# A cross-attention and state-space kernel: the second transpose of 26 row-tile pairs is taken from TensorE and given to VectorE and DMA

## The chip, the cores and the metric

The kernel runs on one core of one Trainium2 chip. The metric is the device time of one execution in microseconds (us), lower is better. TensorE (PE) multiplies matrices and can also transpose; VectorE (DVE), ScalarE (ACT) and GpSimd (POOL) work on vectors; SyncE (SP) issues nearly all DMA transfers. Each engine works through its own queue in order, and a waiting instruction holds up all that stands behind it in that queue.

## The reference, cut to what matters

All arrays are fp32. T = 4096 query rows, S2 = 3202 key rows, H = 512, 8 heads of 64.

```python
x  = layernorm(builder_state, g1, beta1)          # 4096 x 512
base_n = layernorm(base_state, g1, beta1)         # 3202 x 512
x  = residual + mha(x, base_n, W_qkv, b_qkv, W_o, b_o)   # softmax attention, 8 heads
residual = x
xn = layernorm(x, g2, beta2)
U  = (xn @ W_in.T + b_in) @ Bmat                  # 4096 x 64
s_t = silu(s_{t-1} @ A.T) + U[t]                  # a scan over the 4096 rows
ssm_out = states @ Cmat
out = residual + ssm_out + (program_probs.mean(1) @ W_prog.T + b_prog)
```

Two steps need rows turned into columns, because a matmul contracts over partitions: the normalized query rows before the Q projection, and the normalized attention output (`xn`) before the product with W_in and Bmat.

## The kernel before, in words

A first stage (to about 216 us) normalizes the 26 chunks of keys, computes K and V for all heads and writes them to DRAM. Then comes the main stage: 8 blocks of 512 query rows (Q = 0..7), each with 4 head pairs (hp) and 2 halves of 256 rows, so 64 units. A unit goes through 13 steps of 256 keys. A step has eight 64x256 matmuls `s<-q,k` (`scores`, L639), one exponential on ACT (`weights`, L709), one addition into a running sum (`add`, L717, on DVE, or on POOL for steps 2, 6 and 10), and eight matmuls `po<-p,v` (`product`, L749). At the end of a unit POOL folds the sum (`fold`, L724), PE sums it over partitions (`sums`, tile pd, L767), and DVE inverts it (L802) and scales the output. The last 80 us or so hold the scan.

Beside the units run two chains per block, each in two pairs of 128-row tiles:

- `queries` (L866), for the block to come: load x, mean and variance on DVE (`stats`), factors on POOL, `scaled` on ACT (L855, tile xh), then `turn`: eight 128x128 PE transposes into two PSUM tiles (L282, tile tp_x) and two ACT copies to the tile xn (L305). Later, four `heads` pieces (L307) multiply xn by the Q weights: per head pair two accumulation groups of four 128x256 matmuls (L312).
- `project` (L914), for the block that has ended: load x, add a bias row on POOL, `outs` on PE (`pa`, L933), `x1` on DVE, `stats`, `factors`, `mod` on POOL (L947, the row that is stored), `scaled` on ACT, `store`, then `turn` (tile tp_y), two copies (L978) and `inputs`: eight 128x128 matmuls (tile pu, L984), whose result ACT writes to u (L992).

The order of each queue is not written by hand: class `Plan` takes pieces with an engine, an assumed cost in ns, the pieces they come after, a due time in steps of 2150 ns, and counted rings of buffers (`m` = 2 PSUM banks, `x` = 4 row tiles, `xn` = 2, `x1` = 2, ...). It plays the pieces through once and emits them in the order in which they start there. On the chip only that order and the semaphores remain. K and V loads are issued inside the `scores` pieces, 10 and 6 steps ahead; each waits until the buffer it takes (13 per kind) was last read. PE switches between 128-row work (`turn`, `heads`, `outs`, `inputs`) and 64-row work (`scores`, `product`, `sums`, `sample`); the planner charges each switch.

Of the kernel before, what the change touches and what calls it, by code (L numbers as in the profile page):

```python
# [20 lines left out]
P = 128  # L21
NC = H // P
NCH = 26
CK = 128
NDC = NCH // 2
# [144 lines left out]
def xattn_ssm_kernel(  # L170
# [117 lines left out]
    xnp = actx.enter_context(tc.tile_pool(name="xnp", bufs=2))  # L288
# [18 lines left out]
    def heads(Q, hp, xns):  # L307

        pq = m_tile([P, 512], f"pq_{Q}_{hp}")
        for half in range(2):  # L310
            for i in range(NC):
                nc.tensor.matmul(  # L312
                    pq[:, half * QU : (half + 1) * QU],
                    wq[:, i, hp * P : (hp + 1) * P],
                    xns[half][:, i, :],
                    start=(i == 0),
                    stop=(i == NC - 1),
                )
        yield
        t = qp.tile([P, QB], F32, tag="q", name=f"q_{Q}_{hp}")  # L320
        nc.scalar.activation(  # L321
            t, pq, AF.Identity, bias=bias[:, hp : hp + 1], scale=HD**-0.5
        )
        qt[Q, hp] = t

    first_xns = []

    def first_queries(x0):

        xns = []  # L330
        for half in range(2):
            xn = xnp.tile([P, NC, QU], F32, tag="xn", name=f"xn_0_{half}")
            xns.append(xn)
            for t in range(NT // 2):
                name = f"x{half * QU + t * P}"
                last = normalize(x0[:, half * (NT // 2) + t, :], P, name, later=True)
                yield
                yield
                xh = last()
                yield  # L340
                yield
                for _ in turned(xn, xh, t, name):
                    yield
                yield
                yield
        first_xns.extend(xns)
        pieces = heads(0, 0, xns)
        next(pieces)
        for _ in pieces:
            yield  # L350
        yield
# [422 lines left out]

    def output(w):
        Q, hp, half = w["at"]
        o = o_t[Q, hp, half] = op.tile([P, QU], F32, tag="o", name=f"o_{w['name']}", bufs=12)
        nc.scalar.copy(o, w["po"][:, 0, :QU])  # L778

    def join(w):  # L780
        o = o_t[w["at"]]
        nc.vector.tensor_tensor(o, w["po"][:, 1, :QU], o, ALU.add)  # L782

    def finish(w, i, d, plan):
# [5 lines left out]
        def denominators(k):  # L790
            if k == 0:
                w["rd"] = op.tile([P, QU], F32, tag="rd", name=f"rd_{name}", bufs=2)
            to = w["pd"][k][:, :QU] if k else w["rd"]
            nc.scalar.activation(
                to, w["pd"][k][:, :QU], AF.Copy, accum_out=rises[:, 3 * i + k : 3 * i + k + 1]
            )

        def whole():
            nc.vector.tensor_tensor(w["rd"], w["pd"][1][:, :QU], w["rd"], ALU.add)
# [35 lines left out]
    def norm_pieces(plan, ks, gets, d, after, names, gives):  # L835
# [21 lines left out]
        for t, (k, v) in enumerate(zip(ks, vs)):  # L857
# [5 lines left out]
                     [] if t else ["xh", "xh"], [("fs", (*k, "stats")), gives[t]])  # L863
        return vs

    def queries(plan, Q, d):  # L866

        xns, copied = [], []
        for half in range(2):
            ks = [("query", Q, half * 2 + t) for t in range(2)]  # L870
            at = [Q * QB + half * QU + t * P for t in range(2)]
            k2, vs, w = ("queries", Q, half), [{}, {}], {}

            def load(v, r):
                v["x"] = xp_.tile([P, H], F32, tag="x", name=f"x_{r}", bufs=4)
                nc.sync.dma_start(v["x"], x[r : r + P, :])

            for t in range(2):
                plan.add((*ks[t], "load"), "SP", 60, partial(load, vs[t], at[t]), [from_(d - 2 * STEP)],
                         d - 2 * STEP, ["x"])  # L880
            nv = norm_pieces(plan, ks, [lambda v=v: v["x"] for v in vs], d, [(*k, "load") for k in ks],
                             [f"x{r}" for r in at], [("x", (*k, "load")) for k in ks])

            def turn(half=half, nv=nv, at=at, w=w):
                xn = xnp.tile([P, NC, QU], F32, tag="xn", name=f"xn_{Q}_{half}")
                xns.append(xn)
                w["turns"] = [turned(xn, nv[t]["xh"], t, f"x{at[t]}") for t in range(2)]
                for one in w["turns"]:
                    next(one)

            plan.add((*k2, "turn"), "PE", 1050, turn, [(*k, "scaled") for k in ks], d + 4 * STEP,
                     ["m", "m", "xn"], [("xh", (*ks[0], "scaled"))])
            for t in range(2):
                plan.add((*ks[t], "copy"), "ACT", 560, lambda t=t, w=w: next(w["turns"][t], None),
                         [(*k2, "turn")], d + 5 * STEP + t, [], [("m", (*k2, "turn"))])
                copied.append((*ks[t], "copy"))
            d += 2 * QSTEP
        head_pieces(plan, Q, range(NC), xns, copied, d, QSTEP // 2,
                    [("xn", ("queries", Q, half, "turn")) for half in range(2)])

    def head_pieces(plan, Q, hps, xns, copied, d, apart, xn_):
        for hp in hps:
            v = {}

            def head(v=v, hp=hp):
                v["heads"] = heads(Q, hp, xns)
                next(v["heads"])

            plan.add(("heads", Q, hp), "PE", 3700, head, copied, d, ["m", "q"], xn_)
# [4 lines left out]
    def project(plan, Q, halves, d, index):  # L914

        for half in halves:
# [3 lines left out]
            now = plan.ALONE if Q == NQB - 1 else 0  # L920

            def load(v, r):
                v["x"] = xp_.tile([P, H], F32, tag="x", name=f"xr_{r}", bufs=4)
                nc.sync.dma_start(v["x"], x[r : r + P, :])
# [16 lines left out]
            def x1_(v, r):  # L941
                v["x1"] = xp_.tile([P, H], F32, tag="x1", name=f"x1_{r}")
# [10 lines left out]
            for t in range(2):  # L953
                plan.add((*ks[t], "load"), "SP", 60, partial(load, vs[t], at[t]), [from_(d - 4 * STEP)],
                         d - 4 * STEP + t, ["x"])
# [3 lines left out]
                     ["m", "m", "x1", "x1"], [("o_", ("output", i)) for i in units_])  # L959
            for t in range(2):  # L960
                plan.add((*ks[t], "x1"), "DVE", 680, partial(x1_, vs[t], at[t]), [(*k2, "outs")],
                         d + STEP + t, [], [("m", (*k2, "outs"))])
            nv = norm_pieces(plan, ks, [lambda v=v: v["x1"] for v in vs], d + STEP, [(*k, "x1") for k in ks],
                             [f"y{r}" for r in at], [("x1", (*k2, "outs"))] * 2)
            for t in range(2):
                plan.add((*ks[t], "mod"), "POOL", 1280, partial(mod, vs[t]), [(*ks[t], "x1")], d + 2 * STEP,
                         [], [("x1", (*k2, "outs"))])
                plan.add((*ks[t], "store"), "SP", 60, partial(store, vs[t], at[t]), [(*ks[t], "mod")],
                         d + 3 * STEP, [], [("x", (*ks[t], "load"))])
# [10 lines left out]
            def inputs(w=w, at=at):  # L980
                w["pu"] = m_tile([P, P], f"pu_{at[0]}")
                for c in range(NC):
                    for t in range(2):
                        nc.tensor.matmul(  # L984
                            w["pu"][t * NS : (t + 1) * NS], wc[:, c, :], w["xn"][:, t, c, :],
# [3 lines left out]
            def kept(t, w=w, at=at):  # L989
# [10 lines left out]
            plan.add((*k2, "turn"), "PE", 1050, turn, [(*k, "scaled") for k in ks], d + 5 * STEP - now,  # L1000
                     ["m", "m", "xn2"], [("xh", (*ks[0], "scaled"))])
            for t in range(2):
                plan.add((*ks[t], "copy"), "ACT", 560, partial(copy, t),
                         [(*k2, "turn")] + ([(*ks[0], "copy")] if t else []), d + 6 * STEP + t, [],
                         [("m", (*k2, "turn"))])
            plan.add((*k2, "inputs"), "PE", 700, inputs, [(*k, "copy") for k in ks], d + 7 * STEP - now,
                     ["m"], [("xn2", (*k2, "turn"))])
            for t in range(2):
                plan.add((*ks[t], "kept"), "ACT", 280, partial(kept, t), [(*k2, "inputs")],
                         d + 8 * STEP + t, [], [("m", (*k2, "inputs"))])  # L1010
# [53 lines left out]
    def last_fetch():  # L1064

        for g in range(2):
            r = LAST + g * P
            t = xp_.tile([P, H], F32, tag="x", name=f"xr_{r}", bufs=4)
            nc.sync.dma_start(t, x[r : r + P, :])
            xl.append(t)  # L1070

    def open_scan():
# [5 lines left out]
        one = xnp.tile([P, 8, NCK], F32, tag="xn", name="scan_1")  # L1078
# [4 lines left out]
        two = xnp.tile([P, 1024], F32, tag="xn", name="scan_2")  # L1083
# [175 lines left out]
    def last_rows(plan, d):  # L1259
# [9 lines left out]
        def x1_(g):  # L1269
            if g == 0:  # L1270
                wide()
            v["x1"][g] = xp_.tile([P, H], F32, tag="x1", name=f"x1_l{g}")
# [75 lines left out]
        for g in range(2):  # L1348
# [3 lines left out]
                     ["x1"] + ([] if g else ["p", "p"]))  # L1352
# [107 lines left out]
    def drain(plan):  # L1460
# [4 lines left out]
        plan.add("fetch", "SP", 500, last_fetch, stored + [("weights", n, NDC - 1)], d, ["x", "x"])  # L1465
# [9 lines left out]
        plan.add("c2", "SP", 200, open_scan, [("heads", NQB - 1, NC - 1)], a0 - 6 * STEP, ["xn", "xn", "q"])  # L1475
# [208 lines left out]
    with tc.manual_schedule():  # L1684
        for g in range(AHEAD_K):
            load_k(*steps[g])
        for g in range(AHEAD):
# [3 lines left out]
                s=2, m=2, mt=1, o=1, p=NP, acc=3, extra=4, q=6, x=4, x1=2, xn2=1, fs=2,  # L1691
                xn=2, xh=2, max=2, rd=2, o_=12,
            ),
            dict(q=[("heads", 0, 0)], xn=[("first", half) for half in range(2)]),
        )
        head_pieces(plan, 0, range(1, NC), first_xns, [], 4 * STEP, 4 * STEP,
                    [("xn", ("first", half)) for half in range(2)])
# [109 lines left out]
```

## Time and profile before

| | |
|---|---|
| median of 3 runs | 2023.07 us (2022.85 to 2023.64) |
| the profiled execution's own time | 2022.73 us |
| its span, first to last instruction | 2020.9 us |
| granted TensorE clock, mean | 0.995 |
| busy: PE, DVE, ACT, POOL | 1983.2, 1170.6, 1160.3, 789.3 us |
| PE transposes of x rows and of y rows (L282) | 128 and 120 instructions, 17.7 and 16.4 us busy |
| ACT copies of these (L305, L978) | 32 and 30, 17.3 and 16.1 us |
| DMA packets | 187030, 190.66 MB |
| K and V loads | 432 of 128 KB of each, median 2.2 us to landing |

A row of the profile's table of groups gives line, engine, operation, tiles (out<-in), shape, count, then busy us, mean ns of one instruction, then the engine's idle time before such instructions and what ended it. The engine-over-time view gives start, duration, engine, line, operation and count; the duration of a group of matmuls reaches to the modelled end of the last one, so the pace is read from the starts. fp32 matmuls stand as two instructions each in the trace, transposes as one.

### The profile page before, as it was taken

How to read it: one execution, taken by the hardware profiler on the slowest of the kernel's cores; microseconds unless marked ns; L12 is line 12 of the kernel's file. 1: busy time of each engine (PE TensorE's matmuls, PEld its weight loads, DVE VectorE, ACT ScalarE, POOL GpSimd, SP SyncE). 2: the span in 40 equal slices, each digit the busy share in tenths (PEclk: the TensorE clock that was granted, in tenths of full speed). 3: DMA queues.
4: the chain of work that ended last, by engine and by line, in shares of the span. 5: the costliest groups of instructions: out<-in, count | busy, mean ns of one | idle time of the engine just before them, and what ended most of it. 6: DMA issues, size and time to landing. Idle time of an engine off the chain costs nothing.

```text
span 2020.9 us, 66912 instructions
## 1 busy us (share of the span) xinstructions
PE 1983.2 (98%) x29534; PEld 1324.9 (66%) x29534; DVE 1170.6 (58%) x1481; ACT 1160.3 (57%) x1530; POOL 789.3 (39%) x631
## 2 busy tenths in 40 slices
PE   8999999999999999999999999999999999999996
PEld 4445676776677667766677667766776667766764
DVE  4321366566665666566656666566656665666575
ACT  2233566566665566556656666556655665665653
POOL 2111244235533453245523553345324552345424
PEclk9999999999999999999999999999999999999998
DMA  5632322122222322122222222232212322444475
GB/s 169 192 99 68 99 79 83 54 80 90 88 67 78 97 79 67 55 62 93 81 59 80 90 88 67 78 96 79 67 55 62 93 81 59 144 136 129 130 208 192
DMA packets 187030, 190.66 MB, mean 94 GB/s; under 512 B 20904, under 2 KB 160168, under 8 KB 186732
## 3 DMA queue, kind: packets, MB, share of 16 engines
q1 hardware_dynamic: 182184, 178.62, 29.4%
q10 hardware_dynamic: 4548, 7.67, 1.2%
q8 instruction: 235, 3.85, 0.8%
q14 instruction: 63, 0.52, 0.1%
HBM read 156.32 MB, written 29.88 MB: 92 GB/s over the span
## 4 chain that ended last, share of the span: by engine, by line
PE 78%; DVE 10%; POOL 7%; issue 3%; ACT 1%; DMA 1%; DVEq 0%; POOLq 0%; ACTq 0%
PE po L749 27%; PE s L639 27%; DVE acc L717 6%; PE pq L312 5%; PE pk L588 4%; PE pv L555 4%; POOL acc L717 4%; PE pa L933 4%; PE pd L767 1%; DVE rd L802 1%; ACT p L709 1%; PE tp_x L282 1%; DVE acc L703 1%; POOL acc L724 1%; PE sm L657 1%
## 5 line engine op out<-in xcount | busy, mean ns | idle before, releaser
L709 ACT ACTIVATE p<-s,shifts 128x1024 f32<-128x1024 f32 (+1 forms) x832 | 894.1, 1081 | 522.8 <-PE s L639 510.4
L717 DVE TENSOR_TENSOR acc<-p,acc 128x1024 f32<-128x1024 f32 (+1 forms) x515 | 620.0, 1204 | 406.9 <-POOL acc L717 310.6
L639 PE MATMUL s<-q,k 64*64 64x256 f32 x12800 | 841.4, 378 | 2.7 <-ACT p L709 1.1
L749 PE MATMUL po<-p,v 64*64 64x256 f32 x12800 | 823.2, 376 | 0.0
L717 POOL TENSOR_TENSOR acc<-p,acc 128x1024 f32<-128x1024 f32 x189 | 446.9, 2365 | 809.1 <-DVE acc L717 484.1
L639 PEld LDWEIGHTS s<-q,k 64*64 64x64 f32 x12800 | 483.9, 133 | 217.2 <-issue 21.4
L749 PEld LDWEIGHTS po<-p,v 64*64 64x64 f32 x12800 | 489.5, 133 | 189.0 <-issue 2.2
L724 POOL TENSOR_TENSOR acc<-acc 128x512 f32<-128x512 f32 x64 | 104.5, 1633 | 135.8 <-DVE acc L717 118.0
L717 DVE TENSOR_TENSOR acc<-p,p 128x1024 f32<-128x1024 f32 x64 | 84.6, 1322 | 60.1 <-ACT p L709 54.1
L312 PE MATMUL pq<-xn,wq 128*128 128x256 f32 x512 | 119.0, 385 | 0.0
L802 DVE RECIPROCAL rd<-rd 128x256 f32<-128x256 f32 (+1 forms) x65 | 112.4, 1729 | 2.2
L312 PEld LDWEIGHTS pq<-xn,wq 128*128 128x128 f32 x512 | 94.6, 190 | 23.2 <-issue 11.6
L933 PE MATMUL pa<-wo,o 128*128 128x512 f32 x240 | 107.0, 599 | 0.0
L782 DVE TENSOR_TENSOR o<-po,o 128x256 f32<-128x256 f32 x64 | 27.2, 424 | 128.4 <-ACT o L778 128.2
L555 PE MATMUL pv<-wv,ct 128*128 128x512 f32 (+1 forms) x208 | 96.4, 616 | 1.0 <-ACT ct L523 0.7
L588 PE MATMUL pk<-ct,wk 128*128 128x512 f32 (+1 forms) x224 | 88.8, 549 | 0.0
L321 ACT ACTIVATE q<-pq,bias 128x512 f32<-128x512 f32 x32 | 22.0, 687 | 108.6 <-PE pq L312 108.6
L933 PEld LDWEIGHTS pa<-wo,o 128*128 128x128 f32 x240 | 44.4, 190 | 56.0 <-issue 55.8
L703 DVE TENSOR_TENSOR acc<-x,acc 2x256 f32<-2x256 f32 x128 | 78.1, 610 | 3.0
L523 DVE COPY ct<-tp_c 128x512 f32<-128x512 f32 (+1 forms) x13 | 8.5, 651 | 105.9 <-PE tp_c L282 105.9
L555 PEld LDWEIGHTS pv<-wv,ct 128*128 128x128 f32 (+1 forms) x208 | 38.3, 193 | 44.5 <-issue 41.7
L588 PEld LDWEIGHTS pk<-ct,wk 128*128 128x128 f32 x224 | 39.2, 190 | 42.6 <-issue 42.6
(213 smaller groups left out, 1224.1 us busy)
## 6 DMA issues: line engine op xcount, KB each, us to landing
k<-kd SPq DMA_DIRECT2D x432, 128.0 KB, 2.2
v<-vd SPq DMA_DIRECT2D x432, 128.0 KB, 2.2
xr<-in_x_dram SPq DMA_DIRECT2D x32, 256.0 KB, 4.5
x1d<-xr SPq DMA_DIRECT2D x32, 256.0 KB, 2.2
x<-in_x_dram SPq DMA_DIRECT2D x28, 256.0 KB, 3.2
cx<-in_ctx_dram SPq DMA_DIRECT2D x25, 256.0 KB, 3.0
vd<-vs SPq DMA_DIRECT2D x25, 256.0 KB, 2.4
kd<-ks SPq DMA_DIRECT2D x48, 128.0 KB, 1.8
```

What stands on the lines that cost most here:

```text
L312: nc.tensor.matmul(pq[:, half * QU : (half + 1) * QU], wq[:, i, hp * P : (hp + 1) * P], xns[half][:, i, :], start=(i == 0), stop=(i == NC ...
L555: nc.tensor.matmul(pv[h * HD : h * HD + n, :H], ct[:, k, o : o + n], wv[:, k, :], start=(i == 0), stop=(i == NC // parts - 1), skip_group_ ...
L588: nc.tensor.matmul(pk[:, :n_g], wk[:, i, hp * P : (hp + 1) * P], ct[:, i, :n_g], start=(i == 0), stop=(i == NC - 1),)
L639: nc.tensor.matmul(s[k0 : k0 + HD, a, b, :], kts[(*w["at"][:2], c)][r, b * CK + k0 : b * CK + k0 + HD], q[r], start=True, stop=True, skip_ ...
L703: nc.vector.tensor_tensor(to[r], t[r], to[r], ALU.add)
L709: nc.scalar.activation(t[:, :, :nb, :], w["ps"][c][:, :, :nb, :], AF.Exp, bias=w["shift"])
L717: engine.tensor_tensor(w["acc"][:, :, :nb, :], t[:, :, :nb, :], before[:, :, :nb, :], ALU.add)
L724: nc.gpsimd.tensor_tensor(acc[:, :, 0, :], acc[:, :, 0, :], acc[:, :, 1, :], ALU.add)
L749: nc.tensor.matmul(w["po"][a * HD : (a + 1) * HD, k, :QU], vts[Q, hp, c][r, b, a * HD : (a + 1) * HD], t[r, a, b, :], start=(c == 0 and b ...
L782: nc.vector.tensor_tensor(o, w["po"][:, 1, :QU], o, ALU.add)
L802: nc.vector.reciprocal(w["rd"][:, part], w["rd"][:, part])
L933: nc.tensor.matmul(v["pa"], o_t[Q, c, half][:, t * P : (t + 1) * P], wo[:, c, :], start=(c == 0), stop=(c == NC - 1),)
```

## The change

For 26 of the 29 pairs that these chains handle in the main stage (the query pairs of blocks 1 to 6, and the output pairs of blocks 0 to 6), `turn` and the two copies are replaced. After `scaled`, two DVE instructions (`flip`) transpose each 128x512 tile in 32x32 blocks, from xh into the pair's own row tile (x or x1), interleaving the blocks of the two tiles. Then 16 DMA transfers on SP (four `move` pieces of four) carry blocks to their partitions: each takes 32 partitions x 4 x 64 numbers, that is 128 pieces of 256 bytes, 32 KB. The columns of xn (512 wide now, one tile for both halves) then stand in mixed order: 32 rows of the first tile, 32 of the second, and so on. `inputs` reads its columns with a stride to undo that; for the queries of blocks 1 to 6 the mixed order stays through scores, exponentials and products, and is undone where ACT and DVE read `po` and `pd` from PSUM (`output`, `join`, `denominators`, `whole`). `heads` has one group of four 128x512 matmuls in place of two groups of four 128x256. Row tiles are now kept in pairs (rings x = 2, x1 = 1, xn = 1: the same bytes), a row pair's `flip` also waits for both `mod` pieces, its `store` is planned after its `flip`, and `inputs` is due 16 steps after `outs` instead of 7. The query blocks 0 and 7 and the last block's output pair keep PE transposes.

```diff
-        for half in range(2):
-            for i in range(NC):
-                nc.tensor.matmul(
-                    pq[:, half * QU : (half + 1) * QU],
-                    wq[:, i, hp * P : (hp + 1) * P],
-                    xns[half][:, i, :],
+        for i in range(NC):
+            nc.tensor.matmul(
+                pq,
+                wq[:, i, hp * P : (hp + 1) * P],
+                xn[:, i, :],
...
+    def rows_of(w, t, of_queries=False):
+        if not mixes(w["at"][0]):
+            return t
+        return mixed(t, slice(None)) if of_queries else t.rearrange("p (t a r) -> p t a r", t=2, r=TB)
...
-        nc.scalar.copy(o, w["po"][:, 0, :QU])
+        nc.scalar.copy(rows_of(w, o), rows_of(w, w["po"][:, 0, :QU], True))
...
-            plan.add((*k2, "turn"), "PE", 1050, turn, [(*k, "scaled") for k in ks], d + 4 * STEP,
-                     ["m", "m", "xn"], [("xh", (*ks[0], "scaled"))])
-            for t in range(2):
-                plan.add((*ks[t], "copy"), "ACT", 560, lambda t=t, w=w: next(w["turns"][t], None),
+            if mixes(Q):
+                for t in range(2):
+                    plan.add((*ks[t], "flip"), "DVE", 720,
+                             lambda t=t, v=v, nv=nv: flip(v["x"], nv[t]["xh"], t),
+                             [(*k, "scaled") for k in ks], d + 4 * STEP + t, [], [("xh", (*ks[0], "scaled"))])
+                for a in range(P // TB):
+                    plan.add((*ks[0], f"move{a}"), "SP", 2600, partial(move_, a),
+                             [(*k, "flip") for k in ks] + ([(*ks[0], "move0")] if a else after),
+                             d + (5 + 4 * a) * STEP, [] if a else takes, [free])
...
+    def flip(pair, xh, t):
+        nc.vector.transpose(
+            pair.rearrange("p t h -> p (t h)").rearrange("p (g t r) -> p t g r", t=2, r=TB)[:, t],
+            xh.rearrange("p (g r) -> p g r", r=TB),
+        )
+
+    def move(xn, pair, a):
+        n = 2 * TB
+        of = pair[a * TB : (a + 1) * TB].rearrange("p t h -> p (t h)").rearrange(
+            "p (c b k) -> p b c k", b=P // TB, k=n
+        )
+        for b in range(P // TB):
+            nc.sync.dma_start(xn[b * TB : (b + 1) * TB, :, a * n : (a + 1) * n], of[:, b])
+
+    def mixed(of, t):
+        return of.rearrange("p (a t r) -> p t a r", t=2, r=TB)[:, t]
+
+    def mixes(Q):
+        return 0 < Q < NQB - 1
...
-                         [], [("x1", (*k2, "outs"))])
-                plan.add((*ks[t], "store"), "SP", 60, partial(store, vs[t], at[t]), [(*ks[t], "mod")],
+                plan.add((*ks[t], "store"), "SP", 800, partial(store, vs[t], at[t]),
+                         [(*ks[t], "mod" if last else "flip")], d + 3 * STEP, [], [("x", (*ks[0], "load"))])
...
-                            w["pu"][t * NS : (t + 1) * NS], wc[:, c, :], w["xn"][:, t, c, :],
+                            w["pu"][t * NS : (t + 1) * NS], wc[:, c, :],
+                            w["xn"][:, t, c, :] if last else mixed(w["xn"][:, c, :], t),
...
+                for t in range(2):
+                    plan.add((*ks[t], "flip"), "DVE", 720, lambda t=t, w=w, nv=nv: flip(w["x1"], nv[t]["xh"], t),
+                             [(*k, of) for k in ks for of in ("scaled", "mod")], d + 5 * STEP + t, [],
+                             [("xh", (*ks[0], "scaled"))])
+                for a in range(P // TB):
+                    plan.add((*ks[0], f"move{a}"), "SP", 2600, partial(move_, a),
+                             [(*k, "flip") for k in ks] + ([xn2] if a else []), d + (6 + 2 * a) * STEP,
+                             [] if a else ["xn2"], [("x1", (*k2, "outs"))])
```

## The prediction

> **What bounds the kernel now.** I read the page's totals first, then the PE idle time by engine waits, then PE's queue over time, and only then the other engines around the row pairs.
>
> From the page: the span, busy time by engine, and the 40 slices of PE and of its granted clock.
>
> ```profile
> span 2020.9 us, 66912 instructions
> ...
> PE 1983.2 (98%) x29534; PEld 1324.9 (66%) x29534; DVE 1170.6 (58%) x1481; ACT 1160.3 (57%) x1530; POOL 789.3 (39%) x631
> ...
> PE   8999999999999999999999999999999999999996
> ...
> PEclk9999999999999999999999999999999999999998
> ```
>
> PE is busy in nearly every slice at full clock; 30 of its 38 us of idle lie in the first 245 us and the last 61 (view by stage). In the main stage only one wait of PE's matmuls on another engine recurs, pd (the sum over partitions) waiting for POOL's fold, seen in the waits by PE and by its weight loads:
>
> ```profile
> PE pd L767 <- POOL acc L724: 4.9, 6, 0.8
> PEld pd L767 <- POOL acc L724: 11.0, 12, 1.3
> ```
>
> So PE work taken from the main stage should come off the end, unless it turns into a wait of that kind. The groups by shape that the change touches:
>
> ```profile
> L312 PE MATMUL pq<-xn,wq 128*128 128x256 f32 x512 | 119.0, 385 | 0.0
> L933 PE MATMUL pa<-wo,o 128*128 128x512 f32 x240 | 107.0, 599 | 0.0
> L282 PE MATMUL tp_x<-ident,xh_x 128*128 128x128 f32 x128 | 17.7, 279 | 0.0
> L282 PE MATMUL tp_y<-ident,xh_y 128*128 128x128 f32 x120 | 16.4, 280 | 0.0
> L305 ACT COPY xn<-tp_x 128x512 f32<-128x512 f32 x32 | 17.3, 588 | 1.7 <-PE tp_x L282 1.7
> ```
>
> **What goes: the PE transposes.** One `turn` in PE's queue over time:
>
> ```profile
> 914.88 1.91 PE L639 MATMUL s<-q,k 64*64 64x256 f32 x32
> 916.72 1.09 PE L282 MATMUL tp_y<-ident,xh_y 128*128 128x128 f32 x8
> 917.74 1.58 PE L639 MATMUL s<-q,k 64*64 64x256 f32 x24
> 919.13 1.04 PE L749 MATMUL po<-p,v 64*64 64x256 f32 x16
> ```
>
> Sixteen 64x256 records take 0.865 us where nothing interrupts, 0.054 each. So the first s ends at 914.88 + 32 x 0.054 = 916.61, and the second would have begun, counted back from po, at 919.13 - 24 x 0.054 = 917.83. The turn with both switches of tile size costs 1.22 us; another (931.4 to 932.6) costs 1.18. In the built order of PE the main stage holds 29 turns before and 3 after, and none shared its switches with other 128-row work, so 26 x 1.2 = 31.2 us go. That the transposes disappear is thus certain; only what follows is open.
>
> **`heads`.** A piece is 16 records in 3.65 us (pq from 810.53 to the next s at 814.18). Eight records of 128x512 at 107.0/240 = 0.446 us are 3.57; in one run of 16 pa records (902.47 to 909.53) they are 0.441, hence 3.53. I take 0.1 x 32 = 3.2 us.
>
> **`inputs`.** The same 16 records of 128 columns, read in runs of 32. Scan matmuls of 32 columns with a stride of 16 bytes (L1098 zl, 231 ns) last as long as the 64 contiguous ones of sm L676 (230 ns), so I take nothing; between 0 and double (14 x 1.0 us) lie the ends.
>
> **PE's added waits.** 20 matmuls (6 of `heads`, 14 of `inputs`) now wait for 6 to 8 DMA semaphores. Semaphore instructions on PE's queue last 51 ns at the median in the trace, so at most 20 x 7 x 0.051 = 7 us; the one product before with six waits (227.67) starts 0.05 us after the s work ahead of it (225.89 + 1.73), since PE's queue runs ahead of its array. I take 1.5.
>
> **Flips.** 52 DVE instructions on 128x512. Nearest rows with 512 elements per partition on DVE: bn_stats 673 to 695 ns, x1 681; the far end is three times that, as ACT's strided write of u (L992, 479 ns for 128 elements) is against its 364 for 256. I take 0.7: 36 us of DVE, which has 800 us idle. What matters is who stands behind a flip. In DVE's new order the row flips come after the ninth add, and the second query pair's flips right after its stats, ahead of adds 11 and 12, the fold and pd. In the trace DVE stands idle just there:
>
> ```profile
> 919.65 1.22 DVE L717 TENSOR_TENSOR acc<-p,acc 128x1024 f32<-128x1024 f32 x1 [5.43 <-POOL acc L717]
> ...
> 976.45 2.02 DVE L717 TENSOR_TENSOR acc<-p,acc 128x1024 f32<-128x1024 f32 x2 [4.21 <-ACT xh_x L855]
> ```
>
> First place: the second xh_y is ready at 916.15 (ACT 915.34 + 0.81), the flips run 916.2 to 917.6, and the add waits for POOL until 919.6 anyway. Only one stats of x now precedes the fold, so POOL reaches the fold some 2 us sooner, while PE reaches pd 1.5 us sooner (turn and inputs gone from between, 2.4; one scores group more, 0.86). Second place: four flips, POOL's factors and tenth add begin 1.45 us later (975.5), the flips of x end at 978.6 instead of add 11 starting at 976.45, and the fold ends near 981.8 against 979.8; pd stood at 983.49 and comes to about 982.0. Both are level within 0.5 us. I take 2 us for new pd waits in all, with ends of -5 (today's waits vanish) and +34 (26 pairs x today's longest, 1.3).
>
> The Trainium skill's page Vector Engine (DVE) Microarchitecture Reference, section 3.8, says the transpose mode sustains one element per cycle per lane. By the skill's 0.96 GHz that would be an estimated 0.53 us plus a start, the near end of these rows; no trace here shows it.
>
> **ACT.** 52 copies at 0.59 go (31 us); ACT waits 510 us for scores in the table of waits, so nothing is gained. `output` and `denominators` read PSUM in runs of 32: free, or at three times as much 48 x 0.75 us for each of three on ACT, which has 860 us idle. The two DVE reads, 0.42 each now, likewise fall in its idle.
>
> **Moves on SP.** 416 DMAs of 32 KB. SP's queue:
>
> ```profile
> 913.59 0.66 SPq L1021 DMA_DIRECT2D k<-kd  x1
> 914.34 0.41 SPq L1029 DMA_DIRECT2D v<-vd  x1
> 914.85 0.38 SPq L1021 DMA_DIRECT2D k<-kd  x1
> ```
>
> An issue costs 0.4 us, so 16 take 6.4; loads of 128 KB overlap although each lands 2.2 us after issue. Behind a waiting move stand K and V loads, whose buffers are free about 13 steps (28 us) before use: a block of SP of 11.8 us (the longest wait of `store` for POOL, L950) leaves PE untouched today. That wait shrinks, since `store` now stands after the flip. Between the last move's due time and its reader lie 4 steps (8.6 us) for `inputs` and 7 for `heads`. I take nothing.
>
> **Sum.** 2023.07 (the profiled execution, 2022.73, is 0.34 under the median) - 31.2 - 3.2 + 1.5 + 2 = **1992.2**, given as 1992.
>
> **Rivals.**
>
> *The flip is slow and DVE becomes the bound* (slower). Beside the second place's four flips there is no room left, at the others about 2 us. At 1.4 us a flip, 6 such places lose 2.8 us and the other 14 pairs up to 1.4: 36 us, which eats the gain (2028). At 2.1: 73 us, 2065. It decides from about 1.4 us on. For it: DVE is in order and pd already waits on that chain. Against it: all rows of 512 elements stay under 0.7.
>
> *The moves come late.* If the 16 went one after the other, each landing (2.2 us) before the next, a row pair would need 35 us where `inputs` is due 10 steps (21.5 us) after the first: 13.7 us x 14 = 192 us, about 2180. It decides from 1.34 us per move. Against: the loads above overlap. The skill's page DMA: Bandwidth & Descriptors (Rules for kernel authors) speaks for it: coalesce, transfers under 64 KB are mostly overhead. By that rule, 32 KB in 256-byte pieces is a poor transfer; the trace's smallest K loads (64 KB, 1.9 us) show only that such overhead is latency that overlaps.
>
> *Half the gain is given back in pd waits.* The full 7 us on semaphores and 1.3 us at each of 14 row pairs (18): 2023.07 - 34.4 + 25 = 2014.
>
> **Chances.** Forecast 0.72 (1982 to 2002: up 10 for the waits, down 10 for today's pd waits and idle at changed places); half given back 0.13 (2002 to 2019, of which 0.01 within 0.2%); slow flip 0.10, of which 0.03 within 0.2%; late moves 0.05. Within 0.2% (4 us, about what a measurement of this kernel can tell from no change) 0.04 in all, faster 0.84, slower 0.12. The range leaves out slow flips, late moves and little more: 1982 to 2015.
>
> **What would show it.** tp_x at 32 and tp_y at 8 records; PE busy down by about 34 us; pq at 256 records near 0.445 us; flips near 0.7 us; pd waits on POOL near today's 11 us; moves issued at 0.4 us and K loads without a wait on PE's side. Wrong if flips exceed 1.4 us, if pu or pq waits for DMA, or if pd's waits grow by tens of us.

## The result, and the profile after

The changed kernel takes 2033.59 us (median of 5 runs, 2031.61 to 2036.71), against 2023.07 before: a ratio of 1.0052 with a 95% interval of 1.0038 to 1.0067. It is slower by half a per cent, where 1992 was forecast. The profiled execution took 2036.71 us, 3.1 above the median; before's lies 0.3 below its own, so the profiles differ by 14.0 us and the medians by 10.5.

The page of the changed kernel (span, busy time, PE over 40 slices, TensorE's granted clock, DMA packets):

```profile
span 2034.9 us, 66527 instructions
...
PE 1967.0 (97%) x29070; PEld 1258.4 (62%) x29070; DVE 1210.8 (60%) x1533; ACT 1134.3 (56%) x1478; POOL 796.7 (39%) x631
...
PE   8999999999999999999999999999999999989996
...
PEclk9999999999999999999999999999999999999998
...
DMA packets 246935, 204.28 MB, mean 100 GB/s; under 512 B 80809, under 2 KB 220073, under 8 KB 246637
```

PE's busy time fell by 16.2 us, half of what was expected, and one slice (1781 to 1831 us) now shows an 8. The clock row is the same as before: what is lost below is too short to show in slices of 51 us. The groups that the change touches, by shape (busy us, mean ns of one | idle time of the engine before them):

```profile
L312 PE MATMUL pq<-xn,wq 128*128 128x512 f32 x256 | 118.3, 605 | 0.0
L932 DVE STREAM_TRANSPOSE x<-xh_y 128x512 f32<-128x512 f32 x28 | 18.2, 690 | 15.8 <-ACT xh_y L857 15.8
L932 DVE STREAM_TRANSPOSE x<-xh_x 128x512 f32<-128x512 f32 x24 | 15.6, 689 | 22.8 <-ACT xh_x L857 19.3 <-DMA v<-vd 3.4
L283 PE MATMUL tp_x<-ident,xh_x 128*128 128x128 f32 x32 | 4.8, 278 | 1.5 <-ACT u L1051 1.5
L283 PE MATMUL tp_y<-ident,xh_y 128*128 128x128 f32 x8 | 1.3, 286 | 0.0
```

The transposes are gone as planned, and a flip takes 0.69 us. But DVE stood still before flips for 38.6 us. PE's waits in the main stage of the changed kernel (us in total, times, longest):

```profile
PE s L635 <- ACT p L705: 15.6, 17, 2.7
PE pd L763 <- POOL acc L720: 9.8, 4, 6.9
PE pu L1042 <- DVE x L1000: 4.8, 1, 4.8
PE pu L1042 <- DMA xn<-x: 4.5, 2, 3.2
```

Before, only pd had 4.9 us and s 1.1. To put this into one account I summed the gaps between PE's matmul records from 216 to 1945 us, and took the time at which the last scores matmul ends (1955.1 us before, 1969.2 after). PE's gaps grew from 8.5 to 38.8 us (+30.3). And the trace's clock records show something that the kernel before never had in this stage: six stretches, 27.3 us in all, at half the TensorE clock. PE was busy for 23.5 us of them, so 11.7 us are lost. With 30.3 + 11.7 lost and an end 14.1 us later, PE's own work fell by 27.9 us. Two such stretches, as busy time of PE, PEld, DVE, ACT and POOL in a window, with the granted clock ahead of the last two columns. The records give 941.9 to 945.3 us for the first and 1829.4 to 1836.2 for the second; the windows reach a little beyond, hence 0.53:

```profile
942.10:945.50 3.40, 3.40 (x40) 2.12 (x36) 2.06 (x3) 1.11 (x1) 1.26 (x2) 0.53 0.32 58
...
1829.00:1836.00 7.00, 3.77 (x36) 2.29 (x40) 5.81 (x8) 1.73 (x5) 4.54 (x2) 0.53 0.03 9
```

**A gap that comes once per block.** SP's queue of the changed kernel, between the two loads of one query pair (start, duration, count):

```profile
899.43 0.38 SPq L880 DMA_DIRECT2D x<-in_x_dram  x1
...
913.92 3.29 SPq L944 DMA_DIRECT2D xn<-x  x4
...
919.31 2.52 SPq L944 DMA_DIRECT2D xn<-x  x4
...
924.15 6.13 SPq L944 DMA_DIRECT2D xn<-x  x8
...
930.96 0.43 SPq L880 DMA_DIRECT2D x<-in_x_dram  x1
```

Before, the two loads were issued together. Now the 16 moves of a row pair stand between them. A move takes 0.68 us of SP on average (281.3 us for 416), not 0.4. Between the two loads the 16 moves alone take 11.9 us; for the rest SP waits for buffers and flips or issues other transfers. What follows from the late load, engine by engine:

```profile
933.70 0.69 DVE L845 BATCH_NORM_STATS2 st_x<-x 128x6 f32<-128x512 f32 x1 [2.68 <-DMA x<-in_x_dram]
...
935.90 1.59 POOL L850 TENSOR_TENSOR rstd_x<-rstd_x,neg_half 128x1 f32<-128x1 f32 x1
...
938.56 0.81 ACT L857 ACTIVATE xh_x<-x,nm_x,rstd_x 128x512 f32<-128x512 f32 x1 [3.38 <-POOL nm_x L851]
...
941.00 1.17 PE L635 MATMUL s<-q,k 64*64 64x256 f32 x16 [1.93 <-ACT p L705]
```

Statistics wait for the load, POOL's factors are late and slow, ACT stands at xh with exponentials behind it, and PE finds no free PSUM bank for its scores. The clock record drops to 0.5 at 941.9, a microsecond after PE resumes.

**The last flipped rows.** From 1799 to 1828 us SP issues without a pause, since the last block loads K and V for every unit. The xr loads go out at 1812.3 and 1813.7, behind ten moves:

```profile
1815.25 1.28 POOL L981 TENSOR_TENSOR xr<-xr,rowb 128x512 f32<-128x512 f32 x1 [11.28 <-DMA xr<-in_x_dram]
...
1821.49 3.89 DVE L713 TENSOR_TENSOR acc<-p,acc 128x1024 f32<-128x1024 f32 x3 [9.35 <-POOL acc L713]
...
1832.23 1.13 PE L763 MATMUL pd<-acc,ones 64*64 64x256 f32 x8 [6.92 <-POOL acc L720]
```

### The profile page after: what moved, and what is told of

Same layout as the page of the kernel before. It is cut to its first block, busy times and chain, and to the rows that moved or that the text cites. A ratio compares the mean times of both kernels' runs of the same rounds, so it can differ in the third digit from the quotient of the medians.

```text
span 2034.9 us, 66527 instructions
## 1 busy us (share of the span) xinstructions
PE 1967.0 (97%) x29070; PEld 1258.4 (62%) x29070; DVE 1210.8 (60%) x1533; ACT 1134.3 (56%) x1478; POOL 796.7 (39%) x631
## 4 chain that ended last, share of the span: by engine, by line
PE 70%; DVE 11%; POOL 9%; issue 3%; SPq 3%; ACT 2%; DMA 2%; DVEq 0%; POOLq 0%; ACTq 0%
PE s L635 24%; PE po L745 24%; DVE acc L713 7%; PE pq L312 5%; POOL acc L713 4%; PE pk L584 4%; PE pv L551 4%; PE pa L987 3%; SPq L944 2%; ACT p L705 1%; PE pd L763 1%; DVE rd L804 1%; DMA x<-in_x_dram 1%; POOL rstd_x L850 1%; DVE acc L699 1%
## 5 line engine op out<-in xcount | busy, mean ns | idle before, releaser
L713 DVE TENSOR_TENSOR acc<-p,p 128x1024 f32<-128x1024 f32 x64 | 95.9, 1499 | 40.0 <-ACT p L705 34.3
L312 PE MATMUL pq<-xn,wq 128*128 128x512 f32 x256 | 118.3, 605 | 0.0
L784 DVE TENSOR_TENSOR o<-po,o 128x256 f32<-128x256 f32 x64 | 27.1, 423 | 95.3 <-ACT o L780 94.8
L312 PEld LDWEIGHTS pq<-xn,wq 128*128 128x128 f32 x256 | 46.0, 189 | 57.5 <-issue 57.5
```

Source lines behind the costliest of these rows:

```text
L312: nc.tensor.matmul(pq, wq[:, i, hp * P : (hp + 1) * P], xn[:, i, :], start=(i == 0), stop=(i == NC - 1),)
L713: engine.tensor_tensor(w["acc"][:, :, :nb, :], t[:, :, :nb, :], before[:, :, :nb, :], ALU.add)
```

## The experiments

All were compared with runs of the kernel before on the same chip (2022.6 to 2023.0). Theory A held SP's moves responsible, B the flips on DVE, C something else in the change; D and E are told in the expectations of e3 and e4.

### Each half, and neither

Run e1: the row pairs are turned on PE as before, the query pairs stay flipped.

```diff
-            last = Q == NQB - 1
-            now = plan.ALONE if last else 0
+            last = True
+            now = plan.ALONE if Q == NQB - 1 else 0
```

> The 14 flipped row pairs go back to the PE turn with ACT copies; the 12 query pairs stay flipped and moved. Theory A (SP's queue: 16 moves of a row pair, 0.63 us an issue, stand ahead of the second x load of each query pair, and in the last block ahead of the xr loads): PE gets 14 x 1.2 = 17 us of work back, but the gaps of PE after late loads (five of about 2.2 us, then 6.9 and 4.8, 38.8 us of idle in the main stage against 8.5) and the windows at half clock (27 us, 13.7 lost) go: about 2034 + 17 - 40 = 2010, within 2005 to 2016. Theory B (the flips and DVE's order are what costs): half of the loss and half of the gain go, about 2028. Theory C (512-wide heads, pair buffers or the strided reads of output and denominators cost): 2040 or more.

Measured: **2005.60, ratio 0.9918 (0.9902 to 0.9935)**, faster than both kernels. PE's main-stage gaps are 7.6 us, no half clock, and its only wait of weight in this stage is the old one, pd for the fold:

```profile
PE pd L763 <- POOL acc L720: 5.6, 7, 0.8
```

The last scores end 17.0 us earlier than before. Without 0.9 of smaller gaps and 0.7 of heads that is 1.28 us for each of 12 turns; against e2 below, which has the same heads and turns all pairs on PE, it is 1.22.

Run e9 is its complement, rows flipped and queries turned on PE:

```diff
-        return 0 < Q < NQB - 1
+        return False
```

> The complement of the run without row flips: the 14 row pairs stay flipped and moved, the 12 query pairs are turned on PE. PE's work falls by 14 x 1.3 = 18 us. If the row pairs alone carry all that is lost (46 us: 2033.6 - 2005.6 and the 18 they save), 2050; if the loss needs both kinds of moves on SP together, 2015 to 2030; if rows alone lose nothing, as the queries alone did, 2004.

Measured: 2056.0 (four runs, 2049.8 to 2064.4; the profile is of the shortest), ratio 1.0178 (1.0148 to 1.0207). The first case: the row pairs carry all of the loss by themselves. Gain and loss add up only roughly (-17 and +33 against +10.5). In its waits the moves' landing stands first, six times:

```profile
PE pu L1042 <- DMA xn<-x: 14.8, 6, 3.0
PE tp_x L283 <- ACT u L1051: 10.4, 6, 2.0
PE pd L763 <- POOL acc L720: 6.9, 1, 6.9
```

Run e2 does both edits, so nothing is flipped or moved.

> No pair is flipped or moved; what is left of the change is the heads of 512 columns, the pair tiles with fewer and larger buffers and their load order. Theories A and B: before less 3.2 us for the heads, about 2020 (2017 to 2023), PE idle in the main stage near 8.5 us and no half clock there. Theory C: slower than before, 2026 or more, with the waits for scores already there.

Measured: 2021.38, ratio 0.9995 (0.9985 to 1.0004). Theory C fell: wide heads, pair tiles and fewer buffers cost nothing. They bring little either: PE's busy time under pq went from 119.0 to 118.3 us.

### The moves: how many, and how large their pieces

Run e3 copies a quarter of a pair straight with one DMA, run e4 with four:

```diff
-            "p (c b k) -> p b c k", b=P // TB, k=n
+            "p (c k) -> p c k", c=NC
...
-        for b in range(P // TB):
-            nc.sync.dma_start(xn[b * TB : (b + 1) * TB, :, a * n : (a + 1) * n], of[:, b])
+        nc.sync.dma_start(xn[a * TB : (a + 1) * TB], of)                                    # e3
+        for b in range(P // TB): nc.sync.dma_start(xn[a * TB : (a + 1) * TB, b], of[:, b])  # e4
```

> As the changed kernel, but each of the four moves of a pair is one DMA of 32 partitions that copies straight, 1-KB pieces, the same bytes: 104 DMAs in place of 416. The output is not the reference's, since the blocks are not moved. Theory A by the count of issues: SP is held 26 x 12 x 0.6 = 190 us less, loads are in time, PE idle in the main stage falls from 38.8 to under 15 us and the half clock nearly goes: 1992 to 2003. Theory D (SP held by the moves' waits for the flips, not by issues): 2022 or more. Theory B: no better than 2028.

> As the changed kernel, but the 16 DMAs of a pair copy straight in pieces of 1 KB (32 partitions each, 32 KB) in place of 256 bytes; the output is not the reference's. The count of issues stays, the pieces are a quarter as many. Theory A by the count of issues: 2030 or more. Theory E (the 256-byte pieces make the issue 0.63 us in place of 0.4, or slow other transfers): the issues fall to 0.4 us and the time to 2015 or less.

Measured: e3 2007.01, ratio 0.9919 (0.9903 to 0.9936), gaps of 19.9 us and no half clock; e4 2025.35, ratio 1.0011 (1.0001 to 1.0021), gaps of 35.0. e3 lies 4 us above A's range and far from D's and B's; e4 lies between A's and E's. Between the two the bytes and the planner's entries, and so the order of every queue, are the same: 312 fewer issues are worth 18 us. Theory E fell in its reason: with pieces of 1 KB an issue still takes 0.65 us on average. Why e4 is nonetheless 8 us better than the changed kernel (its late x load came 5.7 us earlier) was not followed up; its runs spread over 10 us.

### The flips alone

Run e10 is e1 with the 28 row flips added on DVE, into a tile that nobody reads.

```diff
+                for t in range(2 * (Q < NQB - 1)):
+                    plan.add((*ks[t], "flip"), "DVE", 720, lambda t=t, w=w, nv=nv: flip(w["x1"], nv[t]["xh"], t),
+                             [(*k, of) for k in ks for of in ("scaled", "mod")], d + 5 * STEP + t, [],
+                             [("xh", (*ks[0], "scaled")), ("x1", (*k2, "outs"))])
```

> The run without row flips (2005.6: rows turned on PE), and on top of it the 28 row flips on DVE at the place where they stand in the changed kernel, into the pair tile that nobody reads afterwards; no row moves. This prices the flips alone: 28 x 0.69 = 19 us of DVE. Theory A (SP's moves cost): 2005 to 2009. Theory B (a flip that waits for xh at the head of DVE, with adds behind it, costs): 2015 or more, with new waits of pd for POOL or of scores for ACT.

Measured: 2014.04, ratio 0.9956 (0.9940 to 0.9973): 8.4 us slower than e1. That is beyond A's range and just short of B's bound, and B's sign is there: five waits of 1.44 us that e1 does not have.

```profile
PE s L635 <- ACT p L705: 7.2, 5, 1.4
```

So the row flips have a price of their own, though the smaller part.

### The loads' place in SP's queue

Run e5 issues both x loads of a query pair as one step. Run e6 moves the due times of all x and xr loads 30 steps ahead. Run e7 adds to e6 that the rows of block 6 are turned on PE. Run e8 issues these loads from ACT's queue.

```diff
+            plan.add((*ks[0], "load"), "SP", 800, load, [from_(d - 2 * STEP)], d - 2 * STEP, ["x"])  # e5
...
-                         [(*ks[0], "load")] if t else [from_(d - 2 * STEP)], d - 2 * STEP + t, [] if t else ["x"])
+                         [(*ks[0], "load")] if t else [from_(d - 2 * STEP)], d - 32 * STEP + t, [] if t else ["x"])  # e6
...
-            last = Q == NQB - 1
+            last = Q >= NQB - 2                                                                      # e7
...
-                plan.add((*ks[t], "load"), "SP", 800, partial(load, t),
+                plan.add((*ks[t], "load"), "ACT", 60, partial(load, t),                                  # e8
...
-                nc.sync.dma_start(v["x"][:, t], x[at[t] : at[t] + P, :])
+                nc.scalar.dma_start(v["x"][:, t], x[at[t] : at[t] + P, :])                           # e8
```

> As the changed kernel, but the two x loads of a query pair are one step of SP, so that no move stands between them (in the changed kernel the first is issued at 899.4, the second at 931.0, with 16 moves between). Theory A: the chain late load, late statistics, POOL's factors, xh, exponentials goes: five gaps of PE before scores (1.7 to 2.7, 10.8 us) and three windows at half clock (10.2 us, 5.1 lost): 2033.6 - 16 = 2018, within 2013 to 2022; the gaps near 1642, 1832 and 1887 stay. Theory B (POOL and ACT are late because of the flips in DVE's order): 2030 or more, with the five gaps still there.

> As the changed kernel, but the x and xr loads are given due times 30 steps earlier, so that SP issues them ahead of moves whenever their buffer is free; moves and flips stay. Theory A: besides the five gaps, the xr loads of the last stage (POOL waits 26 us for them) come in time, and the gaps of 6.9 and 4.8 us with their half clock (5.1 lost) go too: about 2002 (1997 to 2010). If the last stage is late because SP has no time left there (moves and K and V loads issue back to back from 1812 to 1830), its gaps stay and the time is as with the loads together, near 2018. Theory B: 2030 or more.

> The earlier due times of the loads, and besides the row pairs of the last flipped block (those worked on while the last block's K and V are loaded for every unit) are turned on PE again: two turns of 1.2 us come back, 32 of 416 moves go. Theory A: all of the 30 us of new idle and the 13.7 us of half clock go: 2033.6 - 44 + 2.4 = 1992 (1988 to 1998). Theory C (something else than late loads in the flipped rows): above 2005.

> As the changed kernel, but the x and xr loads are issued on ACT's queue, so that no move stands ahead of them anywhere. Theory A: gaps by late loads go, also in the last stage, where SP is then left with moves and K and V loads: 1998 to 2008, the wait of pu for moves near 1642 and late K and V loads may stay. If not the queue but the traffic of the moves makes loads slow (their time from issue to landing, 3.2 to 3.5 us, grows): 2025 or more.

Measured: e5 **2039.09**, ratio 1.0081 (1.0064 to 1.0097); e6 2021.20, 0.9996 (0.9986 to 1.0005); e7 2017.12, 0.9973 (0.9962 to 0.9984); e8 2049.09, 1.0125 (1.0109 to 1.0142). All four missed theory A's range. e5 and e8 took as long as the other theory said, but without its sign: in e5 the five gaps are gone, and in e8 the loads land about as fast as in the changed kernel (below). e7, above 2005, is what theory C stood for: something besides late loads costs in the flipped rows.

In e5 the loads did go out together (901.8 and 902.2), and the long waits of scores went (6.4 us left, the longest 0.7). But now the statistics and factors of both x tiles stand ahead of the fold (on POOL from 920.6 to 924.6, the fold behind them), and pd waits in their place:

```profile
PE pd L763 <- POOL acc L720: 28.3, 14, 6.9
PE s L635 <- ACT p L705: 6.4, 17, 0.7
```

So the place of one load is a link of the chain, not the cause of the loss. e6 brings 12 us: the last stage's gaps fall to 3.0 and 1.9 us, but pd waits 1.56 us at six places, and pu still waits 8.7 us for moves. In e8 scores wait 39.3 us for exponentials: on ACT a load stands in the same queue as these, and DVE still waited 39.5 us for x. From issue to landing a load took 3.1 to 3.6 us there (medians of xr and x), 3.2 to 3.5 in the changed kernel and 3.2 to 3.9 in e2, which moves nothing: the moves' traffic does not slow loads.

### A move with 5 issues

Run e11 lets each pair go through DRAM: four DMAs write its quarters there with the blocks in order, one reads it back.

```diff
-                for a in range(P // TB):
+                for a in range(2):
...
-        for b in range(P // TB):
-            nc.sync.dma_start(xn[b * TB : (b + 1) * TB, :, a * n : (a + 1) * n], of[:, b])
+        nb = P // TB
+        if a == 0:
+            turns[id(pair)] = dram.tile([nb, TB, NC, nb, n], F32, name=f"turn_{next(count)}")
+            for g in range(nb):
+                nc.sync.dma_start(
+                    turns[id(pair)][:, :, :, g, :].rearrange("b p c k -> p c b k"),
+                    pair[g * TB : (g + 1) * TB].rearrange("p t h -> p (t h)").rearrange("p (c b k) -> p c b k", b=nb, k=n),
+                )
+            return
+        nc.sync.dma_start(xn, turns[id(pair)].rearrange("b p c a k -> (b p) c (a k)"))
```

> As the changed kernel, but a pair is moved through DRAM: four DMAs of 128 KB write its quarters in 256-byte pieces with the blocks already in order, one DMA of 512 KB reads it back: 5 issues in place of 16, and the pair's buffer is free after the four. SP spends 26 x 11 x 0.6 = 170 us less on issues. Theory A (issues): as with 104 straight moves or better, 1996 to 2008. If the second trip (2 to 3.5 us from issue to landing, on the same queue, behind which K and V loads stand) costs, 2015 or more with waits of pu or pq for DMA.

Run e12 adds e6's due times.

> The way through DRAM with 5 issues, and the due times of the x and xr loads 30 steps earlier. With issues few and loads early, the waits of scores and of pu should go, and the waits of pd that the early loads showed (1.57 at seven places, against 0.8 before) stay: main-stage idle 15 to 20 us, no half clock, 1996 to 2006. If early loads cost by themselves (factors of x ahead of the fold on POOL), it is slower than the same kernel without them.

Measured: e11 2012.04, ratio 0.9962 (0.9946 to 0.9979); e12 2009.80, 0.9934 (0.9918 to 0.9951). Both lie some 4 us above the range expected, and e11's five runs spread from 2009.8 to 2019.1 (the profile is of the shortest). The same result as the changed kernel's, with 130 issues for 416, is 21.6 us faster. Not all of that must be the issues: e11 also frees a pair's buffer sooner, and with other pieces the planner orders all queues anew. The second trip was no burden in e11: neither pu nor pq waited for DMA there. What stayed, besides the pd waits that e12 shows again, are many short waits:

```profile
PE s L635 <- ACT p L705: 11.1, 19, 1.0
PE po L745 <- DVE o L784: 3.6, 4, 1.1
```

### What is left

Runs e13 and e14 put the query pairs 10 steps later (in the changed kernel and in e11), e15 puts e11's row flips and moves 4 steps later, e16 does both. In e17 and e18 the planner reckons 2.6 us for POOL's factors in place of 1.05 (again in the changed kernel and in e11), so that it orders xh later on ACT.

```diff
-                queries(plan, Q + 1, i * NDC * STEP)
+                queries(plan, Q + 1, (i * NDC + 10) * STEP)                                        # e13, e14, e16
...
-            [(*k, of) for k in ks for of in ("scaled", "mod")], d + 5 * STEP + t, [],
+            [(*k, of) for k in ks for of in ("scaled", "mod")], d + 9 * STEP + t, [],              # e15, e16
...
-                             [(*k, "flip") for k in ks] + ([xn2] if a else []), d + (6 + 2 * a) * STEP,
+                             [(*k, "flip") for k in ks] + ([xn2] if a else []), d + (10 + 2 * a) * STEP,  # e15, e16
...
-            plan.add((*k, "factors"), "POOL", 1050, partial(factors_, v), [(*k, "stats")], d + 2000)
+            plan.add((*k, "factors"), "POOL", 2600, partial(factors_, v), [(*k, "stats")], d + 2000)  # e17, e18
```

> As the changed kernel, but the query pairs' steps are due 10 steps (21.5 us) later, so that the moves of a row pair and of a query pair no longer fall into the same stretch of SP, and the statistics of x no longer directly behind the row flips. If the loss is that the two meet: the scores' waits (15.6 us) and the half clock behind them (10.2 us at half) shrink, 2010 to 2020; the last flipped rows (gaps of 6.9 and 4.8 near 1832 and 1887) stay as they are. If each row pair is too much by itself: 2030 or more.

> The way through DRAM with 5 issues (2012.0), and the query pairs due 10 steps later. What is left there is 11 us of waits of scores for exps (19 of them) and 3.6 of po. If they come from row flips meeting the query pairs' statistics and factors: 1998 to 2005, with under 5 us of such waits. If not: 2009 to 2015.

> The way through DRAM with 5 issues, and the row flips and moves due 4 steps (8.6 us) later, so that xh is there when a flip comes to the head of DVE's queue (DVE waits 14.9 us for xh_y, 8 times) and adds are not held. If the flips cost by holding DVE's queue: 2000 to 2007. If their 0.69 us themselves or where they push the other work cost: 2009 to 2016.

> Both shifts on the way through DRAM: query pairs 10 steps later, row flips 4 steps later. If all waits go, PE alone sets the time: 2022.7 less 28 to 30 of PE's work = 1993 to 1998. If it is not below 2005, the flipped rows keep a cost on DVE, POOL and ACT that no such shift takes away.

> As the changed kernel; the only edit is in the planner's table: it reckons 2.6 us in place of 1.05 for POOL's three factor instructions (the trace has 1.0 to 3.6 us for them), so that it orders xh later on ACT and does not put exponentials behind an xh that waits. If the waits of scores for exps (15.6 us) come from ACT standing at xh for POOL's factors (20.9 us): they halve at least, and the half clock with them, 2033.6 - 8 - 5 = 2020 (2014 to 2025). The gaps of the last stage by SP stay. If it only moves the wait to the fold on POOL and to pd: no better than 2030.

> The same edit on the way through DRAM with 5 issues (2012.0, 11.1 us of scores waiting for exps, ACT 19.5 us at xh for POOL): 2001 to 2006 if that wait of ACT is what is left; 2010 or more if the work on POOL and DVE around the fold is full, so that pd waits in its place.

| run | us | ratio, interval | PE's gaps | lost to half clock |
|---|---|---|---|---|
| e11, for comparison | 2012.04 | 0.9962 (0.9946 to 0.9979) | 20.7 | 0 |
| e13 | 2075.18 | 1.0259 (1.0242 to 1.0276) | 67.4 | 24.7 |
| e14 | 2023.93 | 1.0008 (0.9998 to 1.0018) | 35.1 | 6.5 |
| e15 | 2018.51 | 0.9977 (0.9967 to 0.9987) | 26.6 | 1.4 |
| e16 | 2023.24 | 1.0000 (0.9990 to 1.0010) | 34.9 | 4.8 |
| e17 | 2067.18 | 1.0223 (1.0206 to 1.0241) | 58.0 | 15.7 |
| e18 | 2010.38 | 0.9936 (0.9919 to 0.9952) | 19.3 | 6.7 |

Five of six are no better than the run they start from, and e18's 1.7 us lie within e11's spread. Neither explanation finds support: moving the pairs apart in time, or the flips later, does not bring the loss back. In e13, e14, e16 and e17 the waits of scores for exponentials grew (to 45.9, 28.3, 28.2 and 25.3 us). In e14 the x loads were in time, and the chain was there all the same: from 554.3 POOL's three factor instructions take 1.25, 1.59 and 0.94 us, xh waits 2.9 us on ACT with exponentials behind it, and PE stands for 2.6. e18 is instructive: the waits of scores for exponentials fell from 11.1 to 0.3 us, and join (L784, DVE) took their place:

```profile
PE po L745 <- DVE o L784: 14.6, 9, 3.0
...
758.24 0.69 DVE L845 BATCH_NORM_STATS2 st_x<-x 128x6 f32<-128x512 f32 x1 [4.29 <-DMA x<-in_x_dram]
...
759.65 0.42 DVE L784 TENSOR_TENSOR o<-po,o 128x256 f32<-128x256 f32 x1
```

DVE stands at statistics whose load is late, and join behind them holds the PSUM bank that po wants. In none of these orders does the wait go; it grows, or another in-order queue takes it over. With rows flipped and moved to their places, no order tried gains more than about 13 us on before. How the rest divides between DVE, POOL and ACT stays open: from 2009.8 (e12) or 2012.0 (e11) it is 12 to 19 us down to the 1993 to 1998 that PE's work alone would give.

## Why the prediction was wrong, step by step

- **Turns (31.2 us) held.** e1 measures 1.22 to 1.28 us for a query turn, 1.2 forecast.
- **Heads (3.2) was over-sized:** 0.7 us of PE's time; e2 as a whole gains 1.2 us on before. The 128x512 records of pq last 0.462 us each (118.3 us for 256), not the 0.441 to 0.446 taken from pa.
- **Inputs (0) held:** PE's busy time under pu is 16.4 us before, and 16.4 in e3 and e11, where it reads the mixed columns. **PE's added semaphore waits (1.5)** were not separated. With heads corrected, PE's work should have fallen by 30.4 us and fell by 27.9.
- **Flips:** the duration (0.7) held to 0.01 us. The cover, "which has 800 us idle", did not: 28 flips cost 8.4 us in e10. I had followed who stands behind a flip at two places, and only for adds and the fold; what became late were the statistics and factors after them, and by these xh and the exponentials on ACT. The Trainium skill's page Vector Engine (DVE) Microarchitecture Reference (section 3.8), which I had weighed, bears on the duration alone: the estimate from its rate, 0.53 us and a start, would leave 0.16 us for the start in the 0.69 measured.
- **Moves on SP (0) is the step that failed.** "An issue costs 0.4 us" came from 128-KB loads; a move takes 0.68, so a pair holds SP 10.8 us, not 6.4. Worse, I named only K and V loads behind the moves. The x and xr loads stand there too, with short leads. The term was put at 0 and measured 18 us (e3 against e4) to 21.6 us (e11 against the changed kernel, with the two other differences named there).
- **pd's waits** grew by 4.9, with 2 forecast and 34 as the upper end. But the waits that decided were of other kinds: scores for exponentials (+14.5) and pu (+9.3, half of it put down to the moves' landing).
- **The clock** was not in the sum at all: 11.7 us, part of the prices above, since e3 and e11 have no half clock.
- **The rivals.** "The moves come late" had the right queue and the wrong mechanism: it priced moves one after the other at the latency of each (decides from 1.34 us a move). They overlap, land in 1.9 us (median), and hold the queue by issue time. Its sign did come: pu waits for moves, 4.5 us in the changed kernel and 14.8 in e9. The Trainium skill's page DMA: Bandwidth & Descriptors (Rules for kernel authors) would have small transfers coalesced. The traces agree in effect: 5 issues for 16 gave 21.6 us. But larger pieces alone left the issue at 0.65 us (e4). "Half the gain is given back in pd waits" is what e6 and e12 show in small: once loads come in time, pd waits 1.56 us per block.

In the account of the profiles: 28.3 us of gaps beyond the 2 foreseen, 11.7 of clock and 5.0 of missing PE work are 45.0. Less 3.1, by which this execution lies above its median, and 0.3, by which before's lies below, that leaves 41.6 for the 41.4 between 2033.6 and 1992.2. By cause, if the prices may be added, the moves (18 to 21.6), the row flips (8.4) and the heads (2.5) make 29 to 33 of the 41.4; what the rest is stays open.

## What to carry to other kernels

Price a DMA step by its issue time on the queue that issues it, read for that very kind of transfer, and list every kind of load that stands behind it with the lead it has. Where the main engine is 98% busy, an idle share of 40% on helpers is no cover: their in-order queues form a chain, and a wait that is removed at one link shows up at the next. And when a change has separable halves, price each: here the 12 query pairs gave 17 us and the 14 row pairs cost 33.

## What the runs showed of the hardware

- **Short gaps halve the TensorE clock.** After PE gaps of 1.93 to 6.92 us in the changed kernel the clock records show 0.5 for 3.4 or 6.8 us. The length of a gap alone does not decide: in e12, of six gaps of 1.55 us two (1135, 1353) were followed by a half-clock stretch; in e14, of six gaps of 2.6 to 2.8 us four. What sets the drops apart is how much of a gap falls into one window of a fixed grid. In each of the 20 profiled runs the half-clock stretches start whole multiples of 3.413 us apart. Cut along this grid, the main stages of these runs have 9769 windows at full clock. In the 68 that a drop follows, PE is idle (by its matmul records) for 1.78 to 3.41 us; in all others for 2.02 at most, and in all but 11 of these for less than 1.78. e12's two gaps make 1.79 us in a window, e14's two without a drop are cut in two by a window's end (the larger parts are 1.77 and 1.66). Full clock comes back after a window with at most 0.71 us idle, and not after one with 0.81. The Trainium skill's page TensorE: Matmul & The Clock Gate (Part 1) has a free-running window of 3.4 us, and the grid agrees with it. By its table the half clock comes after at least one idle window; here a window idle for little over half of its length was enough.
- **A DMA that takes rows out of 32 SBUF partitions needs 0.6 us to issue** (medians), where a K load from DRAM takes 0.33: from SBUF to SBUF 599 ns with pieces of 256 bytes, 588 with 1 KB (e4), 591 with 128 KB in place of 32 KB (e3), and 630 from SBUF to DRAM (e11). It is not SBUF as the source alone: the store of a 128-partition tile to DRAM takes 338 to 382 ns. Whether the 32 partitions or the pieces make the difference was not tested. A read of 512 KB from DRAM takes 0.33 us to issue and lands in 3.7 (e11).
- **POOL's 128x1 power instruction** (L850, for the statistics of x) took 962 ns on average in the changed kernel and 593 in e1. In the changed kernel 16 of the 28 took 0.57 us; the other 12 took 1.40 to 1.59 us, and a DVE add ran beside each of these for at least 1.36 us. That the adds cause it was not tested.
